# The first group's Q, K and V as plain products, in a two-layer graph network on one core

## The chip, the cores and the metric

The kernel runs on one NeuronCore of a Trainium2 chip. A core has TensorE (matrix products), VectorE (DVE, element work), ScalarE (ACT, activations and copies), GpSimd (POOL, element work too) and SyncE (SP), which here issues nearly all DMAs. Each engine runs its own instructions in order and waits on semaphores for the others. The metric is the device time of one execution in microseconds (us). Most executions agree within 0.3%.

## What is computed

The reference takes x with 128 batches of 128 rows and 512 features, and a 0/1 matrix of 128 x 128 for each batch. Layer 0 is attention with 8 heads; layer 1 is a graph attention with one score per pair of rows. After each comes the sum with its input and a layer norm. Everything is 32-bit.

```python
q = (inputs @ Wq + bq).reshape(bs, n, N_HEADS, HEAD_DIM)   # k, v likewise
logits = jnp.einsum('bqhd,bkhd->bhqk', q, k) / np.sqrt(HEAD_DIM)
attn = jax.nn.softmax(jnp.where(mask, logits, NEG_INF), axis=-1)
out = jax.nn.relu(jnp.einsum('bhqk,bkhd->bqhd', attn, v).reshape(bs, n, EMBED_DIM) @ Wo + bo)
x = layernorm(x + out)
Wh = x @ W
e = leaky(Wh @ a1 [:, None] + Wh @ a2 [None, :])            # masked, softmax over the first axis
x = layernorm(x + leaky(attention @ Wh))
```

## The kernel before

**Groups and chains.** Four batches form a group: its transposed input XT is 512 features by 512 rows. Q, K and V of a group are products of 512x512x512 each, and are not computed plainly: a scheme of the Strassen kind is used on two levels. The outer level splits each matrix in 2x2 blocks and needs 7 products instead of 8 (p1 to p7); the inner level does the same once more. So 49 products of 128x128x128 stand for 64. A name (Q, K, V) is done in two chains, of four and of three inner products per outer one. Chain c belongs to group c//6; c%6 is 0 and 1 for Q, 2 and 3 for K, 4 and 5 for V. LAST is the last chain.

**What the scheme needs.** Sums of input blocks: outer ones (`sum_x`, L523 to L526, on GpSimd) and inner ones (`inner_sum`, L500, on either engine). Sums of weight blocks: `Weights.build` (L302) gives eight steps, one for the inner 1, four outer ones (`right_blocks`, L259 to L262), then three inner ones (L291). Reading the products out of PSUM takes copies on ScalarE (`copy_out`, L694 to L700) and adds on VectorE (L715), and at the end of a chain three to six combines (`combine`, L731), each on the engine that its token names.

**Where things live.** The sums of wq stay in SBUF for the whole run. Those of Wk and Wv are built once in memory that other things need later (Wk's becomes that of wo and w1, Wv's is the arena), stored to DRAM (`stores`, L316) and streamed back for every later group through a ring of four tiles (`fetch_until`, L634). In group 0 the products read the blocks of all three in place.

**The opening.** x of the first two batches and Wq's first half are loaded first, then the rest (L1292 to L1304, L1389). VectorE and TensorE turn the rows of x; later inputs are loaded by `load_x` as blocks (four DMAs each, L421) and turned on VectorE (L426). Some transposes of the identity (`keep_busy`) run ahead of the first products. Q is scaled by 1/8 by scaling wq itself on VectorE (L1330, L1334), interleaved with the sums of wq and of the first inputs in a list of 25 steps (`opening`, L1369).

**Order.** The program has no scheduler: one order for all engines is written out as tokens. BEGIN covers the opening up to batch 5, STEADY repeats over the rest, PLAN is the end. Each token calls a method, and the instructions go to their engines in that order. `h` issues the next half step of the chains (one p and what reads it, reads being deferred), `a` and `d` the next deferred read on ScalarE and VectorE, `k` and `k.v` the next combine on GpSimd or VectorE, `q` one more streamed weight, `i1.s1a` an inner sum of group 1 (with .v on VectorE), `g1.0` an outer sum. `s0.` tokens are the softmax of batch 0: scores (L875), masked add (L889), maxima (L898), exponentials (L909), division (L923), a store to DRAM and a fetch back that reorders it (L930, L936), the turn (L942) and the product with V (L955). `z` is the rest of layer 0 for a pair of batches, `b4.` loads and turns of batch 4, `w.` the loads and sums of wo and w1. All of SyncE's DMAs leave in this order too, each only when its data and its target are free.

The half steps come from `sequence` (L605), which starts at chain 0 before the change; the result of a chain is written into one fixed tile for each of Q, K and V (`outputs`).

Of the kernel before, what the change touches and what calls it, by code (L numbers as in the profile page):

```python
# [20 lines left out]
BIG = -1e30  # L21

BEGIN = """
    b4.load.1 h o.0 b0.masks o.2 a o.1 o.3 o.6 h o.4 o.8 o.7 o.9 o.5 o.10 wk.build.0 d o.11
    o.12 o.17 wk.build.1 o.13 o.18 o.15 wk.build.2 o.16 o.14 o.19 o.20 wk.build.4 wk.build.3
    h h o.23 o.21 o.24 o.22 a h a wk.build.5 d wk.build.7 wv.build.0 h h h h wv.build.1 a
    wv.build.2 d k.v wk.store.0 h k.v b6.load.0 b1.cast a k.v k.v k.v k.v h a wk.store.1
    b5.load.2 h a b0.cast b4.turn d q w.bias h wk.build.6 d wv.build.3 b2.masks b7.load.1
    wk.store.3 h h h a h wv.build.4 a a wk.store.2 h h h a b3.cast a b0.mask d k.v b1.mask
    k.v k.v d b6.turn d h h h a b2.cast z1.by b7.turn k.v wv.build.5 h a h h h d b5.turn k.v  # L30
    d a a wv.build.6 wv.build.7 g1.0 d g1.1 g1.2 k.v k.v h h h h d a h k.v q q wv.store.2
    w.load b8.load.2 wv.store.1 b4.masks w.w1_load.1 wv.store.0 wv.store.3 k.v k.v d a h
    s0.scores a s0.add.0 k.v s0.add.1 d s0.reduce s2.scores h h s1.scores g1.3 a h h h h
    w.block.0 a s0.exp.0.1 s0.exp.4.5 d s1.add.1 i1.s1a i1.s1b.v s0.exp.2.3 a b4.cast
    s0.exp.6.7 i1.s2a s0.reciprocals.0 d s1.add.0 b2.mask s0.reciprocals.1 s1.reduce h k a
    s0.divide.2.3 s0.divide.4.5 s0.divide.0.1 s0.divide.6.7 s1.exp.7 h d s2.add.1
    w.w1_load.0 b9.load.0 b10.load.1 s3.scores h h a w.w1_load.3 w.w1_load.9 q s0.store
    w.w1_load.7 a z0.by s1.exp.3.4 b3.mask i1.s2b.v k.v k.v i1.s4a s1.exp.0.1 h h s1.exp.5.6
    a s1.exp.2 s3.add.1 d k.v k.v k.v k w.w1_load.6 b1.residual w.w1_load.5 s0.fetch
    w.w1_load.2 w.w1_load.8 h h s3.add.0 s1.reciprocals.1 s2.add.0 s1.reciprocals.0 d  # L40
    s1.divide.4.5 s2.reduce b8.turn i1.s3a i1.s4b i1.s3b h s1.divide.6.7 b5.cast a
    s1.divide.0.1 s1.divide.2.3 d h h a h h a s3.reduce b10.turn s1.store w.w1_load.4
    b0.residual b11.load.2 b2.residual s1.fetch s2.exp.6.7 s2.exp.2.3 s2.exp.4.5 q d
    s0.transpose w.block.1 a s2.exp.0.1 s3.exp.7 h h h d a k.v k.v s2.reciprocals.0
    s2.reciprocals.1 w.w1_sum.1 b4.mask d w.w1_sum.6 h s2.divide.6.7 s2.divide.0.1 a a
    s3.exp.2 s0.attend h h h s2.divide.2.3 s2.divide.4.5 w.block.3 w.w1_sum.2 s3.exp.5.6 d
    w.w1_sum.3 k.v a s0.copy w.halve s1.transpose s3.exp.3.4 z1.bw h h z0.p1 d
    s3.reciprocals.1 b9.turn w.block.2 w.w1_sum.4 k k k s3.exp.0.1 a s1.attend s1.copy h h
    z0.p2 s2.store d k k q s3.reciprocals.0 k.v q s1.sum.0 a s3.divide.7 a z0.t0
    s3.divide.0.1 s3.divide.5.6 b11.turn s1.sum.1 s1.sum.2 s2.fetch h h q h z0.p6 h  # L50
    s3.divide.2 s3.divide.3.4 q s3.store k.v d q w.w1_sum.0 k.v k q s3.fetch b3.residual q a
    z0.t2 z0.bw h a z0.p5 z0.p7 s2.transpose z0.t3 s1.sum.3 g2.0 b12.load.2 d d q g2.1 h
    z0.p4 q q w.w1_sum.9 h h a a w.w1_sum.8 z0.c22 k.v z0.p3 z0.c21 z0.c11 d b5.mask
    z0.stats.1 h z0.c12 k k.v h s2.attend s4.scores h z0.stats.0 s3.transpose s3.attend k
    g2.2 s2.copy a k z0.rstd.1 z0.rstd.0 s3.copy s4.add.1 s4.add.0 s4.reduce h a d
    z0.apply.1 d s5.scores h h h s4.exp.2.3 s4.exp.6.7 z1.p1 h s5.add.0 s5.add.1 s4.exp.0.1
    s4.exp.4.5 a a h g2.3 s3.sum.2 z0.apply.0 s4.reciprocals.1 s4.reciprocals.0 h d
    s5.reduce i2.s1a i2.s2a.v k.v d s4.divide.2.3 s3.sum.0 s3.sum.1 s4.divide.0.1
    s4.divide.4.5 s4.divide.6.7 z1.t0 a h q z0.store.1 q b6.masks z0.store.0 s5.exp.6.7
    s5.exp.3.4 s5.exp.2 a s5.exp.5 s5.exp.0.1 z1.p6 z1.p2 w.w1_sum.5 i2.s3a.v w.w1_sum.7  # L60
    i2.s1b.v k.v z1.t2 i2.s2b d h h h s4.store z0.fetch_both z1.p5 z1.p7 s5.reciprocals.1
    s5.reciprocals.0 z1.c11 s4.fetch a a s5.divide.2 h h s5.divide.7 s5.divide.5.6
    s5.divide.0.1 s5.divide.3.4 k.v z1.t3 d a b7.cast k.v k.v b12.turn w.w1_sum.10 z1.p4 h
    z1.c22 s4.transpose s3.sum.3 k k i2.s4a i2.s4b w.w1_block.0 s4.attend z1.p3 h h
    z0.transpose.0 z1.c21 z0.transpose.1 z1.stats.1 z1.rstd.1 i2.s3b z0.sum.0 d w.w1_sum.11
    s5.store a w.w1_block.1 z0.sum.1 q z1.c12 d s5.fetch h h z1.stats.0 s5.transpose h
    b6.cast a a s4.copy b13.load.0 d b13.turn b14.load.2 q z1.apply.1 k.v s5.attend s5.copy
    z1.rstd.0 w.w1_block.3 z0.sum.2 w.w1_block.2 k s5.sum.0 s5.sum.1 k z0.sum.3 s5.sum.2
    z1.store.1 b6.mask b7.mask s5.sum.3
"""  # L70

STEADY = {
# [96 lines left out]
def kernel(  # L169
# [293 lines left out]
    def sum_x(g, n):  # L463
        if g not in x_sums:
            begin_sums(g)
        x_sums[g][n]()
# [136 lines left out]
    LAST = 6 * (B // GROUP) - 1  # L603

    def sequence():  # L605
        steps = [(0, name) for name in ("p1", "p2", "p5", "p6")]
        for c in range(LAST + 1):
            steps.append((c, "p7"))
            follow = c + 1 <= LAST
            steps += [(c + 1, "p1")] if follow else []  # L610
            steps += [(c, "p4"), (c, "p3")]
            steps += [(c + 1, name) for name in ("p5", "p6", "p2")] if follow else []
        return steps
# [44 lines left out]
    def group_product(c):  # L658
# [6 lines left out]
            return ps_st.tile([P, 4, P], F32, name=f"st_{role}", tag=tag)[:, :count, :]  # L665

        def weight(n, m):
            if name == "Q" or g == 0:
                return {"Q": wq, "K": wk, "V": wv}[name].inner(m)[:, PLACE[n], :]
            return ring[c, f"p{n + 1}"][:, (0, 1, 2, 0, 3, 1, 2)[m], :]  # L670

        def multiply(p, n, start):
# [102 lines left out]

    def split_step():

        if steps_done[0] >= min(len(all_steps), 42 * (B // GROUP) - 13):
            return
        c, name = all_steps[steps_done[0]]  # L780
        steps_done[0] += 1
        half_step(c, name, True)
        if name == "p3":
            combos.extend(combine(c, comb_engine(c)))
# [3 lines left out]
            INNER[g][0](name, (None, "rest")["ab".index(part)], engine=engine)  # L788

    def comb_engine(c):  # L790
        return nc.vector if c % 6 in (3, 5) or c < 4 else nc.gpsimd

    def pair_product(xs, w, add, home, bias=None, bank=None):

# [531 lines left out]
            nc.tensor.transpose(p[:, c, :], turned[:, c * P : (c + 1) * P], ident)  # L1326
        copy(XT[0][:, :, b * P : (b + 1) * P], p)

    def scale(n):
        nc.vector.tensor_scalar_mul(wq.place(n), wq.place(n), QSCALE)  # L1330

    def scaled_less(n, left, right):

        nc.vector.scalar_tensor_tensor(  # L1334
            wq.place(n), wq.place(left), QSCALE, wq.place(right), op0=ALU.mult, op1=ALU.subtract
        )

    wq_sums = right_blocks([wq.place(n) for n in range(7)])
    begin_sums(0)
    x_inner = INNER[0][0]  # L1340
    turned = [order_features(b) for b in range(2)]
    keep_busy(14)
    transpose_rows(0, turned[0], nc.vector.tensor_copy)
# [1 line left out]
    transpose_rows(1, turned[1], nc.scalar.copy)  # L1345
    turn_biases()
    keep_busy(5)
    scale(0)
    scale(1)
    wq.first(nc.vector, 0, 2)()  # L1350
    x_inner("s1", 0, engine=nc.vector)
    wq.second(nc.vector, 0, 2)()
    x_inner("s2", 0, engine=nc.vector)

    ordered = {}

    def order(b):
        return lambda: ordered.update({b: order_features(b)})

    def rows(b):  # L1360
        return lambda: transpose_rows(b, ordered[b], nc.scalar.copy)

    def sum_of_x(n):
        return lambda: sum_x(0, n)

    def inner_of_x(name, half, engine=None):
        return lambda: x_inner(name, half, engine=engine)

    opening = [  # L1369
        order(2),  # L1370
        rows(2),
        order(3),
        rows(3),
        wq.first(nc.vector, 2, 4),
        lambda: scaled_less(2, 2, 0),
        *[sum_of_x(n) for n in range(4)],
        lambda: scaled_less(5, 3, 2),
        *wq_sums[2:],
        lambda: scale(3),
        wq.second(nc.vector, 2, 7),  # L1380
        inner_of_x("s1", 1, nc.vector),
        inner_of_x("s2", 1, nc.vector),
        inner_of_x("s1", "rest", nc.vector),
        inner_of_x("s2", "rest", nc.vector),
        *wq.others(nc.vector),
        *[inner_of_x(name, half) for name in ("s3", "s4") for half in (None, "rest")],
    ]

    load_blocks(Wv, columns(wv.blocks()), nc.sync)  # L1389
    END = B - GROUP  # L1390
# [28 lines left out]

    class Matrix:  # L1420
        def __init__(self, name, w, engine):
            self.builds = w.build(engine)
            self.stores = w.stores(stored[name, 0], stored[name, 1])

        def build(self, n):
            self.builds[n]()
# [62 lines left out]
    jobs.update({f"z{n}": LayerZero(n) for n in range(2)})  # L1489
    jobs.update({f"b{b}": Batch(b) for b in range(16)})  # L1490
    jobs.update(wk=Matrix("wk", wk, nc.vector), wv=Matrix("wv", wv, nc.gpsimd), w=Late())
    for token in BEGIN.split():
        if token[:2] == "o.":
            opening[int(token[2:])]()
        elif token[0] in "ig" and token[1] in "12":
            g = int(token[1])
            if token[0] == "i":
                common("i" + token[2:], g)
# [224 lines left out]
```

## Time and profile before

| | us |
|---|---|
| median of 3 runs | 2327.47 (2327.29 to 2330.24) |
| the profiled execution | 2328.13 |
| its span in the profile | 2325.5 |
| granted TensorE clock, mean | 0.993 |
| first product of group 0 (L681) | at 8.4 |
| scores of batch 0 (L875) | at 68.1 |
| first product of group 1 (L681) | at 77.4 |
| stores of Wk issued | 31.4 to 52.8 |
| stores of Wv issued | 55.6 to 70.0 |

Each engine's busy time is the union of its instructions; a busy TensorE is not one at its peak, since its products are pipelined and their ends are modelled. Idle time matters only where the chain that ends last passes through it. Times of single instructions are from one profiled execution. The DMA share is the mean busy share of the core's 16 DMA engines.

### The profile page before, as it was taken

Reading aid. Unit: us, or ns where it says so; the run is one execution under the profiler, and the core shown is the slowest. Engines: PE = TensorE matmul, PEld = TensorE weight load, DVE = VectorE, ACT = ScalarE, POOL = GpSimd, SP = SyncE. Lnnn points to the kernel's source line nnn. Section 1 sums busy time; section 2 is a strip of 40 time slices with the busy share of each in tenths; the row PEclk is TensorE's granted clock in tenths of the full one; section 3 lists DMA queues with packets and bytes.
Section 4 is the critical chain, followed back from the end, with each engine's and each line's share of the span. In section 5 each row is a group of like instructions: output and inputs, shape, how many; then the busy total and the mean of one; then the engine's idle time right before and its main releaser. Section 6 shows DMA issues by size and latency. Waiting matters only on the chain.

```text
span 2325.5 us, 53031 instructions
## 1 busy us (share of the span) xinstructions
PE 2264.5 (97%) x17394; PEld 2028.0 (87%) x17394; DVE 2116.6 (91%) x4248; ACT 1665.8 (72%) x5971; POOL 1465.7 (63%) x1735
## 2 busy tenths in 40 slices
PE   5999999999999999999999999999999999999998
PEld 5888988888988888889889889889888889888885
DVE  7998999999999999999999999999999999999977
ACT  1766776777777867767767767767767777777686
POOL 4466666667666666666676666676656666666656
PEclk7999999999999999999999999999999999999999
DMA  6978888888888888878888888888888888888774
GB/s 160 269 209 234 238 249 233 233 232 243 242 241 238 230 236 243 242 240 236 225 246 233 250 238 231 233 240 236 247 238 232 234 244 236 243 238 227 221 217 145
DMA packets 516595, 540.81 MB, mean 233 GB/s; under 512 B 100568, under 2 KB 394336, under 8 KB 516320
## 3 DMA queue, kind: packets, MB, share of 16 engines
q1 hardware_dynamic: 516000, 537.17, 80.8%
q8 instruction: 138, 2.26, 0.4%
q14 instruction: 137, 1.12, 0.2%
q10 hardware_dynamic: 320, 0.26, 0.0%
HBM read 388.96 MB, written 148.31 MB: 231 GB/s over the span
## 4 chain that ended last, share of the span: by engine, by line
PE 58%; DVE 19%; DMA 8%; POOL 5%; SPq 4%; issue 3%; ACT 3%; DVEq 0%; POOLq 0%; ACTq 0%
PE p_y L801 14%; PE st_y L681 14%; PE p_w L801 6%; PE lg L875 6%; PE st_w L681 6%; PE st_x L681 5%; DMA w_n<-wv 4%; DVE pa L942 4%; PE p_x L801 4%; PE p_oT L955 3%; DVE arena L1047 2%; DVE cells L715 2%; PE p_h L1211 2%; DVE st L1003 2%; DMA paz<-pa_dram 2%
## 5 line engine op out<-in xcount | busy, mean ns | idle before, releaser
L909 ACT ACTIVATE pa<-pa,nmax 128x128 f32<-128x128 f32 x1000 | 391.7, 398 | 1.9 <-DVE nmax L898 1.8
L923 ACT ACTIVATE pa<-pa,rs 128x128 f32<-128x128 f32 x1000 | 329.0, 398 | 15.4 <-DVE rs L919 15.2
L1009 POOL TENSOR_SCALAR ve<-mv 128x1 f32<-128x1 f32 x256 | 77.9, 304 | 288.6 <-DVE mv L1005 226.3
L694 ACT COPY cells<-st_y 128x384 f32<-128x384 f32 x288 | 136.2, 473 | 115.8 <-PE st_y L681 102.9
L1024 DVE TENSOR_SCALAR arena<-arena,mv,rstd 128x512 f32<-128x512 f32 x239 | 185.5, 776 | 14.3 <-POOL rstd L1011 14.3
L909 ACT ACTIVATION_READ_ACCUMULATOR pa<-pa,nmax 128x1 f32 x1000 | 194.9, 195 | 0.0
L970 ACT ACTIVATE arena<-p_oT,b_cols 128x128 f32<-128x128 f32 x504 | 144.2, 370 | 64.5 <-PE p_oT L955 60.5
L523 POOL TENSOR_TENSOR x1S<-x1T 128x256 f32<-128x256 f32 x62 | 57.6, 928 | 208.2 <-DVE mf L853 208.2
L1011 POOL TENSOR_TENSOR rstd<-ve,mhalf 128x1 f32<-128x1 f32 x256 | 160.6, 627 | 21.4
L1003 DVE BATCH_NORM_STATS2 st<-arena 128x6 f32<-128x512 f32 x248 | 168.0, 677 | 1.1
L942 DVE STREAM_TRANSPOSE pa<-paz 128x1024 f32<-128x1024 f32 x125 | 154.6, 1237 | 9.6 <-DMA paz<-pa_dram 7.7
L889 DVE TENSOR_TENSOR pa<-lg,mf 128x512 f32<-128x512 f32 x250 | 161.2, 675 | 0.9 <-PE lg L875 0.9
L955 PE MATMUL p_oT<-pa,out_V 128*64 128x128 f32 x2000 | 136.7, 279 | 18.7 <-DVE pa L942 18.7
L694 ACT COPY out_V<-st_y 128x512 f32<-128x512 f32 x128 | 74.5, 582 | 109.5 <-PE st_y L681 109.0
L875 PEld LDWEIGHTS lg<-out_K,out_Q 64*128 64x128 f32 x2048 | 124.2, 187 | 31.9 <-issue 20.4
L875 PE MATMUL lg<-out_K,out_Q 64*128 64x128 f32 x2048 | 148.7, 285 | 0.8 <-DVE out_K L731 0.8
L898 DVE TENSOR_REDUCE nmax<-pa 128x8 f32<-128x1024 f32 x125 | 148.4, 1187 | 0.1
L955 PEld LDWEIGHTS p_oT<-pa,out_V 128*64 128x64 f32 x2000 | 106.7, 136 | 42.0 <-DVE pa L942 33.7
L801 PE MATMUL p_y<-wo_w,x1S 128*128 128x257 f32 x496 | 134.3, 393 | 0.1
L1218 ACT ACTIVATE arena<-p_h 128x512 f32<-128x512 f32 x120 | 71.5, 596 | 87.1 <-DMA out_dram<-arena 59.3
L715 DVE TENSOR_TENSOR cells<-st_w,cells 128x384 f32<-128x384 f32 (+1 forms) x224 | 126.7, 566 | 6.5 <-PE st_w L681 2.9
L801 PE MATMUL p_y<-wo_w,x1T 128*128 128x257 f32 x496 | 131.6, 387 | 0.4 <-ACT arena L812 0.4
(296 smaller groups left out, 7960.2 us busy)
## 6 DMA issues: line engine op xcount, KB each, us to landing
paz<-pa_dram SPq DMA_DIRECT2D x504, 128.0 KB, 3.5
pa_dram<-pa SPq DMA_DIRECT2D x125, 512.0 KB, 3.8
w_n<-wk SPq DMA_DIRECT2D x93, 512.0 KB, 5.9
w_n<-wv SPq DMA_DIRECT2D x93, 512.0 KB, 5.0
w_n<-wk SPq DMA_DIRECT2D x93, 384.0 KB, 4.3
w_n<-wv SPq DMA_DIRECT2D x93, 384.0 KB, 5.6
x_dram<-arena SPq DMA_DIRECT2D x128, 256.0 KB, 2.8
xz<-x_dram SPq DMA_DIRECT2D x240, 128.0 KB, 4.2
```

The costliest lines, as they stand in the source:

```text
L681: nc.tensor.matmul(p[:, index, :], lhs, rhs, start=start and index == 0, stop=True, skip_group_check=True,)
L694: nc.scalar.copy(dst, p)
L715: nc.vector.tensor_add(cells(c)(h, o), p, t)
L801: nc.tensor.matmul(p[:, :width], xs()[n][:, kc, :], w[:, PLACE[n], kc, :], start=start and kc == 0, stop=True, skip_group_check=True,)
L875: nc.tensor.matmul(self.lg[r][:, c, :], q[rows, 2 * (b % 2) + c % 2, c // 2, :], k[rows, 2 * (b % 2) + c % 2, c // 2, :], start=c == 0, st ...
L889: nc.vector.tensor_add(by_head[:, r * NC : (r + 1) * NC], self.lg[r].rearrange("p c (b k) -> p c b k", b=4), mf.unsqueeze(1).to_broadcast( ...
L909: nc.scalar.activation(self.pa[:, :, h, :], self.pa[:, :, h, :], AF.Exp, bias=self.nmax[:, h : h + 1], accum_out=self.sums[:, h : h + 1],)
L923: nc.scalar.activation(self.pa[:, :, h, :], self.pa[:, :, h, :], AF.Copy, scale=self.rs[:, h : h + 1])
L942: nc.vector.transpose(self.paT.rearrange("p h (a i) -> p a h i", i=32), self.paz.rearrange("p a (h k) -> p a h k", k=32),)
L955: nc.tensor.matmul(self.oT[r * HD : (r + 1) * HD, c, :], v[:, c % 2, c // 2, r * HD : (r + 1) * HD], self.paT[:, r * NC + c, :], start=c == 0,
L1003: nc.vector.bn_stats(st, self.src)
L1024: nc.vector.tensor_scalar(self.src, self.src, self.mv[:, 0:1], self.r, ALU.subtract, ALU.mult)
```

## The change

Group 0 no longer goes through the scheme. Its Q, K and V are plain products of the weights as loaded: for Q four output blocks in two halves of 256 columns (`q`), for K four of 512 columns (`k`), for V four batches of 512 columns (`v`). A copy on ScalarE reads each out (`oq`, `ok`, `ov`); Q's copy scales and adds the bias. After Q, wq is scaled in place on ScalarE and its sums are built on VectorE by the same `build` that the others use. The chains begin at chain 6, so 42 half steps go, with the input sums of group 0. BEGIN is written anew: it has 501 tokens instead of 590, with `y.` tokens for the plain products and `wq.` tokens for the scaling and the sums. STEADY and PLAN are as they were.

```diff
     def sequence():
-        steps = [(0, name) for name in ("p1", "p2", "p5", "p6")]
-        for c in range(LAST + 1):
+        steps = [(6, name) for name in ("p1", "p5", "p6", "p2")]
+        for c in range(6, LAST + 1):
...
-        if steps_done[0] >= min(len(all_steps), 42 * (B // GROUP) - 13):
+        if steps_done[0] >= min(len(all_steps), 42 * (B // GROUP - 1) - 13):
...
     def comb_engine(c):
-        return nc.vector if c % 6 in (3, 5) or c < 4 else nc.gpsimd
+        return nc.vector if c % 6 in (3, 5) else nc.gpsimd
...
+    class Group:
...
+        def bank(self, key, n):
+            if key not in self.p:
+                self.p[key] = (
+                    ps_st.tile([P, D], F32, name=f"st_{'ywx'[n]}", tag="abc"[n])
+                    if n < 3
+                    else psum("p_first")
+                )
+            return self.p[key]
+
+        def turned_product(self, name, w, n, cols, start):
+            o, j = divmod(n, 2)
+            p = self.bank((name, n), n)
+            for c in range(NC):
+                block = w.place(2 * o + c // 2).rearrange("p (c f) -> p c f", c=2)
+                nc.tensor.matmul(
+                    p[:, cols],
+                    block[:, c % 2, j * P : (j + 1) * P],
+                    XT[0][:, c, cols],
+                    start=start and c == 0,
...
+        def q(self, n, half):
+            self.turned_product("Q", wq, n, slice(half * 2 * P, (half + 1) * 2 * P), half == 0)
+
+        def oq(self, n):
+            def copy(dst, p, n):
+                nc.scalar.activation(
+                    dst, p, AF.Identity, bias=b_cols[:, 0, n : n + 1], scale=QSCALE
+                )
...
+        def k(self, n):
+            self.turned_product("K", wk, n, slice(0, D), True)
...
+        def v(self, b):
+            p = self.bank(("V", b), b)
+            blocks = wv.low.rearrange("p n (c j) f -> p n c (j f)", c=2)
+            for c in range(NC):
+                nc.tensor.matmul(
+                    p.rearrange("p (o f) -> p o f", o=2),
+                    XT[0][:, c, b * P : (b + 1) * P],
+                    blocks[:, c // 2 : 4 : 2, c % 2, :],
...
     class Matrix:
...
+        def scale(self, n):
+            nc.scalar.mul(self.w.place(n), self.w.place(n), QSCALE)
...
+    jobs.update(wq=Matrix("wq", wq, nc.vector), y=Group())
```

The first tokens of the new BEGIN, up to the first half step of group 1:

```
y.order.3 y.q.0.0 y.order.2 b0.masks y.q.1.0 y.rows.2 y.rows.3 b4.load.1 b6.load.0
b5.load.2 w.bias b2.masks y.q.2.0 y.q.2.1 y.q.1.1 y.oq.1 y.k.3 y.k.1 y.k.2 b4.turn
b1.cast y.q.3.0 y.q.0.1 b0.cast y.oq.2 b7.load.1 y.q.3.1 b1.mask wk.build.0 b6.turn
b5.turn wk.build.1 b3.cast b0.mask wk.build.2 wk.build.3 y.ok.2 b2.cast wq.scale.0
y.oq.0 wq.scale.1 wq.scale.2 y.ok.1 y.ok.3 wq.scale.3 wk.build.4 wk.build.5 y.k.0 y.ok.0
y.oq.3 s0.scores wk.build.6 b7.turn wk.build.7 b2.mask b3.mask s1.scores g1.0 g1.2
...
s0.exp.0.1 s0.exp.6.7 b4.cast s0.exp.4.5 i1.s1a.v wk.store.2 y.v.1 wk.store.3 s0.exp.2.3
b5.cast q q y.v.0 y.v.2 y.v.3 i1.s3a.v s1.reduce wq.build.4 s0.reciprocals.0
s0.reciprocals.1 s0.divide.4.5 s0.divide.2.3 i1.s2a wq.build.3 i1.s4a.v wq.build.5
s1.exp.5.6 s0.divide.0.1 h
```

## The prediction

> **What bounds the kernel now.** I read the page first, then the windows of 20 us, then the waits of TensorE, then the chain of waits, then the timelines of the opening.
>
> The page's busy times and slices:
> ```profile
> PE 2264.5 (97%) x17394; PEld 2028.0 (87%) x17394; DVE 2116.6 (91%) x4248; ACT 1665.8 (72%) x5971; POOL 1465.7 (63%) x1735
> ...
> PE   5999999999999999999999999999999999999998
> ...
> PEclk7999999999999999999999999999999999999999
> ```
> TensorE is the bound everywhere except in the first slice of 58 us, where it is half idle and its granted clock is low. Whatever shifts the moment at which TensorE is kept full shifts the end. The windows (busy of PE, PEld, DVE, ACT, POOL, then clock, DMA share, GB/s) say how far the opening reaches:
> ```profile
> 0.00:20.00 20.00, 9.93 (x57) 8.10 (x57) 10.97 (x22) 3.92 (x8) 7.17 (x11) 0.87 0.86 201
> 20.00:40.00 20.00, 11.34 (x62) 10.37 (x62) 19.86 (x21) 3.34 (x11) 15.85 (x10) 0.70 0.54 146
> 40.00:60.00 20.00, 12.98 (x90) 12.86 (x91) 15.72 (x20) 5.13 (x12) 7.51 (x4) 0.74 0.52 152
> ...
> 80.00:100.00 20.00, 16.55 (x142) 15.14 (x141) 19.20 (x46) 18.56 (x77) 8.63 (x8) 1.00 1.00 231
> 100.00:120.00 20.00, 18.57 (x147) 17.21 (x147) 17.88 (x43) 11.80 (x39) 10.88 (x11) 1.00 0.96 272
> ```
> Two stages: up to 60 us TensorE waits and VectorE is full from 20 us on while the DMA engines are half idle; from 80 us VectorE is full and the DMA share is at 1. The waits of TensorE up to 77.4 us (the end of the first group's V) name the causes:
> ```profile
> PE st_y L681 <- ACT cells L694: 9.7, 1, 9.7
> PE st_w L681 <- DVE inner_s L500: 5.3, 1, 5.3
> PE st_w L681 <- DVE wq L291: 2.6, 1, 2.6
> PE st_w L681 <- DMA wo_w<-in_L_gnn_Wk_dram: 2.4, 1, 2.4
> ```
> The 9.7 us is a VectorE wait in disguise, as the chain shows: the copy waits for the combines of Q (L731).
> ```profile
> 36.97 5.05 DVE out_Q L731 x4
> ...
> 44.09 2.30 DVE out_Q L731
> 46.49 0.49 ACT cells L694
> 47.02 4.64 PE st_y L681 x20
> ...
> 91.61 6.45 DMA xz<-in_x_dram
> 98.08 4.86 DMA paz<-pa_dram
> 103.06 1.25 DVE pa L942
> ```
> Later in the same chain transfers end last: the fetch of the softmax of batch 1 goes out at 95.19 and VectorE gets it at 103.06.
>
> **What the Trainium skill says.** "TensorE: Matmul & The Clock Gate", section "What's actually happening": TensorE has two clocks, half rate after an idle window, full after about 3.4 us of sustained work. The trace agrees: the 5-us windows show 1.00 up to 15 us, 0.50 from 15 to 30 and from 45 to 50, each time after a wait. "SBUF — State Buffer", section "Who interferes with whom": a VectorE instruction with two SBUF inputs and a GpSimd one that reads SBUF block each other. It agrees: two 128x256 combines took 0.87 us at 94.59 with GpSimd idle, and three took 3.58 us at 36.16 with GpSimd full. "DMA: Bandwidth & Descriptors", section "Issuing engines are not separate DMA queues": all issues share 16 engines. Here that shows as the 4.86 us that a 128-KB fetch took beside the weight traffic.
>
> **The change part by part.**
> *Where both programs meet again.* The remaining order of every engine is identical from TensorE instruction 470 (387 in the changed program), VectorE 225 (176) and DMA issue 160 (160). In the trace these points lie at 148.9 us, 157.3 us and about 152 us. I call them the joint; 42 half steps (six chains) go, and the steady loop starts at the same step. So the question is by how much the joint moves.
>
> *TensorE's own work rises.* A 128-column product is two records at 0.222 us (eight st_x records 0.89 us in the chain), a 256-column one 0.43 us (four p_y records 0.86), a 512-column one 0.86 us (two p_h records 0.86). Out: 6 chains with 147 products, 32.6 us. In: 32 of 256 and 32 of 512 columns, 13.8 + 27.5 = 41.3 us. Cost 8.7 us at full clock.
>
> *TensorE's waits in the opening go.* The first product is possible when Wq's first half lands, 7.9 us (where L1330 starts now). Two products groups of 4x0.43 give 11.4; eight transposes 12.3; Wq's second half is there at 12.8 (VectorE's wait ends then); three groups of 1.73 give 18.0; Wk is there by 17.6. Three K groups of 3.45 give 28.4, three Q halves 33.6. K 0 needs the bank that the Q 0 copy frees, and on ScalarE that copy stands behind the first in-place scaling of wq, which must wait for the last Q read: scaling 0.5 and copy 0.6, so K 0 starts at 34.8 and ends at 38.3; two more copies 39.6. Both scores (1.09 each) 41.8, V 16x0.86 = 13.8: 55.6 us. TensorE never rests for long, so I take full clock. Now the same point is 77.4. TensorE is 22 us ahead, with one score product (1.1 us) less done.
>
> *VectorE.* 49 instructions fewer up to the joint: 42 adds of L715 and L731 (0.42 to 0.69 us alone) and five scalings of wq go, two block sums for wq come: some 27 us less. Ten input turns, Wk's builds and wq's builds remain. First stop: the input of batch 4, which is issued after Wv, adj (18.6) and lands near 22.5 us. From there turns (0.7 each) and eight Wk builds (0.69, four of 0.68, three of 1.05) run to 35 us; wq's scaling ends at 37.5; builds, two masked adds and maxima of two batches (0.68, 0.68, 1.2), sums of group 1 beside GpSimd: 54.8 us. Then it waits for V's end (batch 8's turn takes the buffer of the first group's input) and for the score of batch 2: the first add into group 1's Q comes at 60.5 us. It comes at 86.57 now. From there to the joint I count 122 instructions against 123, of the same kinds within 1 us. That stretch is 70.7 us long, and VectorE was busy for 97% of it. Were VectorE alone the limit, the joint would come at 131, 26 us earlier.
>
> *The DMA queue.* Bytes are unchanged: 33 MB up to the joint. SyncE issues in order. Six input batches now go before the first Wk store; that store needs five builds, 30.4 us (31.4 now), the other three by 34.8 (now 52.8). wo and W1 share Wk's memory, so their loads wait for the stores to be read, about 44. Wv's builds overwrite the blocks that the V products read, so GpSimd starts them at 55.8 and takes 15.3 us (as at 30.79 to 46.09 now): 71.1. The queue waits for them twice, at its first Wv store (64) and its last (71.1); behind that stand the fetch of batch 1's softmax, residuals, streamed weights and the store of batch 2. Batch 1's fetch thus leaves at 71 (95.19 now), still 24 us early, but from 64 on Wv's stores, batch 1's store and the fetch bring 4.2 MB, 15.7 us at 270 GB/s: landing near 80 where VectorE would want it at 77. Behind it 3.4 MB to batch 2's fetch, 12.7 us: 92.7 against 86; batch 3, 2.2 MB more, 101 against 97. So transfers are late by 4 to 7 us. I take 6. (From 60 to 155 us the trace moves 244 GB/s at a share of 88%, so 276 at a full one; I take 270.) The total says the same: 33 MB at 270 GB/s is 122 us, to which the early gaps (about 8 us) and some later ones come; a joint at 131 leaves nothing over.
>
> *Other edits.* ScalarE takes 12 copies of 128x512 (0.6) and 4 scalings (0.5) and loses 32 smaller ones (0.31 to 0.59): about 5 us less, and it is idle for half of this stretch. The edit of comb_engine does nothing: chains below 4 are no longer stepped, and each combine's engine stands in its token. GpSimd's sums for group 0 (eight at 1.4 to 2.1 us) go, those for group 1 move ahead of Wv's builds.
>
> *Sum.* 26 minus 6: the joint 20 us earlier. Behind it TensorE is the bound (98% busy from 157 to 297 us), so the lead stays. The profiled execution took 2328.13, its span 2325.5; it lies 0.7 above the median of 2327.47. 2328.1 - 20 = 2308, from the median 2307.5.
>
> The costs not shown: a Q scaling on ScalarE of 128x512 from SBUF has no row; between 0.4 (VectorE's L1330) and 0.6 (copies from PSUM), I take 0.5: 4 of them, at most 0.4 us either way. The late transfers are 0 to 14 us (nothing excludes that the queue holds further issues back). TensorE's clock in the opening: if it falls to half for one stretch as it does now, 3 to 5 us; if not, 0, which I take.
>
> **Rivals.**
> 1. *Transfers keep up.* For it: the store of Wk leaves 15 us earlier and the half-idle DMA from 20 to 60 us is filled. Against it: shares of 1 between 80 and 125. The joint moves 26 us: 2301.5.
> 2. *The DMA queue becomes the bound.* For it: SyncE is stopped four times (Wk stores, wo's memory, batch 8's turn, Wv stores) and the traffic is squeezed from 152 into about 130 us. Then two thirds of the lead go, and 8 us remain: 2319.5.
> 3. *Nothing to see.* The joint is held at about 148 by the total of transfers with gaps of 26 us: 2325.
> 4. *Slower.* The queue stands at the last Wv store, which waits for GpSimd, which waits for V and shares its port with a full VectorE. Batch 1's fetch, now issued at 95.19, stands behind. Wv's builds would have to take 40 us instead of 15.3 (each doubled and more by VectorE's lock) for this to decide; each us later than 95 costs one: with 50 us of builds 2338. Against it: with GpSimd full VectorE is what suffers in the trace (3.58 us for three combines), the builds took 1.3 to 2.2 us each.
>
> That the sums are not built meanwhile is excluded by the order: TensorE has both scores and V between k and the first group-1 product.
>
> **How the numbers follow.** The forecast, 20 us off with its own range of 2303 to 2313, has 0.47; rival 1 0.21, rival 2 0.21, rival 3 0.05, rival 4 0.06. A measurement of this kernel tells 0.2%, 4.7 us, from no change. Faster: 0.47 + 0.21 + 0.21 = 0.89; same 0.05; slower 0.06. The range runs from 2299, rival 1 with 2.5 us to spare, to 2320, which takes in most of rival 2.
>
> **What would show it.** Right: the first plain product at 8 us and V's end near 56; the first score near 40; clock 1.00 from 8 us on; the last Wv store at about 71; VectorE's first add into out_Q near 60; the joint on VectorE near 137; waits on fetches of paz between 75 and 105. Wrong: TensorE at half clock from 15 to 40 us, a first score after 50, Wv stores after 80, or a joint later than 148; and a lead at the joint that is lost again before 300 us would refute that TensorE bounds what follows.

## The result and the profile after

| | before | after |
|---|---|---|
| median of 6 runs, us | 2327.34 (2325.08 to 2330.24) | 2306.28 (2304.29 to 2309.14) |
| profiled execution, us (span) | 2328.13 (2325.5) | 2304.29 (2302.5) |
| first product of group 0 / first score / end of group 0's V, us | 8.4 / 68.1 / 81.2 | 7.8 / 37.6 / 53.6 |
| first product of group 1, us | 77.4 | 54.9 |
| first add into group 1's Q, us | 86.57 | 60.99 |
| joint on VectorE (first masked add of batch 6), us | 158.2 | 133.3 |

The ratio of the medians is 0.991, with a 95% interval of 0.9898 to 0.9923: 21 us less, 18 to 24 by the interval. The forecast was 2307.5.

The page of the changed kernel, busy times and slices:
```profile
PE 2265.1 (98%) x17228; PEld 2013.5 (87%) x17228; DVE 2076.6 (90%) x4199; ACT 1661.2 (72%) x5955; POOL 1443.9 (63%) x1723
...
PE   9899999999999999999999999999999999999998
...
PEclk9999999999999999999999999999999999999999
```
TensorE's busy time is the same as before to 0.6 us, although its granted clock is now full from the start; VectorE has 40 us less to do. The first slice went from 5 to 9 tenths (the second from 9 to 8): the gain is there. The windows (us, busy of PE, PEld, DVE, ACT and POOL with their instructions, clock, DMA share, GB/s) show it more closely:
```profile
0.00:20.00 20.00, 18.09 (x85) 14.68 (x86) 2.75 (x9) 3.82 (x6) 0.72 (x7) 1.00 0.87 204
20.00:40.00 20.00, 19.32 (x85) 11.42 (x84) 13.16 (x18) 6.88 (x15) 4.90 (x4) 1.00 0.79 217
40.00:60.00 20.00, 18.13 (x74) 9.77 (x73) 16.75 (x27) 12.09 (x50) 11.97 (x8) 1.00 1.06 290
...
80.00:100.00 20.00, 19.90 (x167) 18.30 (x168) 18.20 (x48) 12.14 (x38) 10.01 (x10) 1.00 0.93 304
100.00:120.00 20.00, 18.23 (x138) 15.49 (x138) 19.56 (x47) 16.41 (x64) 12.18 (x15) 1.00 0.70 202
```
In the first 60 us TensorE and VectorE have changed places: TensorE is busy for 55.5 us (34.3 before), VectorE for 32.7 (46.6 before). The waits of TensorE in the first 56 us answer to the 9.7, 5.3, 2.6 and 2.4 us of before:
```profile
PE p_busy L1320 <- POOL ident masks.py:199: 1.3, 1, 1.3
PE st_y L681 <- ACT out_V L1416: 1.3, 1, 1.3
PE lg L875 <- ACT out_K L1395: 0.7, 1, 0.7
PE st_y L1364 <- DMA wq<-in_L_gnn_Wq_dram: 0.4, 1, 0.4
```
No wait for VectorE is left among them. What ends last now is in the chain of waits (start, length, what; the long steps up to batch 1's attention):
```profile
17.78 5.71 DMA adj<-in_adj_dram
...
26.29 4.22 DMA adj<-in_adj_dram
...
36.56 8.64 DMA wk<-wo_w
...
46.21 5.53 DMA wo_w<-in_L_gnn_Wo_dram
51.76 6.73 DMA wo_w<-in_L_gnn_W_dram
...
63.20 6.74 DMA wv<-arena
...
74.25 4.53 DMA paz<-pa_dram
78.80 1.26 DVE pa L942
80.10 1.09 PE p_oT L955 x16
```
Before, this stretch of the chain was VectorE's combines and TensorE's products. Now each long step up to 78.8 us is a transfer, and the last Wv store and batch 1's fetch stand in it, as the forecast's part on the DMA queue had them. Behind the joint the lead was kept: batch by batch, VectorE's transpose of the softmax (L942) comes 23.8 to 25.4 us earlier from the fifth to the 124th of 128, and 23.0 us earlier for the last four.

### The profile page after: what moved, and what is told of

Its sections match the earlier page's. It is cut to its first block, busy times and chain, and to the rows that moved or that the text cites. A ratio compares the mean times of both kernels' runs of the same rounds, so it can differ in the third digit from the quotient of the medians.

```text
span 2302.5 us, 52596 instructions
## 1 busy us (share of the span) xinstructions
PE 2265.1 (98%) x17228; PEld 2013.5 (87%) x17228; DVE 2076.6 (90%) x4199; ACT 1661.2 (72%) x5955; POOL 1443.9 (63%) x1723
## 4 chain that ended last, share of the span: by engine, by line
PE 58%; DVE 19%; DMA 9%; POOL 6%; SPq 3%; issue 3%; ACT 2%; DVEq 0%; POOLq 0%; ACTq 0%
PE p_y L801 14%; PE st_y L681 13%; PE lg L875 6%; PE p_w L801 6%; PE st_w L681 6%; PE st_x L681 5%; DVE pa L942 4%; PE p_x L801 4%; DMA w_n<-wv 3%; PE p_oT L955 3%; DVE arena L1047 3%; DVE cells L715 2%; DVE st L1003 2%; PE p_h L1211 2%; DVE arena L1024 2%
## 5 line engine op out<-in xcount | busy, mean ns | idle before, releaser
L923 ACT ACTIVATE pa<-pa,rs 128x128 f32<-128x128 f32 x1000 | 329.2, 397 | 14.4 <-DVE rs L919 14.3
L942 DVE STREAM_TRANSPOSE pa<-paz 128x1024 f32<-128x1024 f32 x125 | 154.5, 1236 | 8.5 <-DMA paz<-pa_dram 6.1
L1218 ACT ACTIVATE arena<-p_h 128x512 f32<-128x512 f32 x120 | 71.5, 596 | 87.8 <-DMA out_dram<-arena 60.5
L801 PE MATMUL p_y<-wo_w,x1S 128*128 128x257 f32 x496 | 134.3, 393 | 0.2
L801 PE MATMUL p_y<-wo_w,oS 128*128 128x256 f32 x504 | 129.8, 380 | 0.4 <-ACT y L812 0.4
```

Source lines behind the costliest of these rows:

```text
L801: nc.tensor.matmul(p[:, :width], xs()[n][:, kc, :], w[:, PLACE[n], kc, :], start=start and kc == 0, stop=True, skip_group_check=True,)
L923: nc.scalar.activation(self.pa[:, :, h, :], self.pa[:, :, h, :], AF.Copy, scale=self.rs[:, h : h + 1])
L942: nc.vector.transpose(self.paT.rearrange("p h (a i) -> p a h i", i=32), self.paz.rearrange("p a (h k) -> p a h k", k=32),)
```

## The experiments

How much two numbers may differ before it means something: the changed kernel was profiled twice, with the joint at 133.3 and 135.0 us, spans of 2302.5 and 2304.9 us, and medians 21.1 and 20.3 us under before's on the same chip. I take 20.7 us as its gain. A joint under 3 us away, or a median under 2 us away, says nothing. In the table "cost" is 20.7 less the kernel's own gain over before beside it.

| run | edit | median | before beside it | ratio (95%) | joint | cost, us |
|---|---|---|---|---|---|---|
| e1 | +8.7 us TensorE, opening | 2313.94 | 2328.33 | 0.9935 (0.9921 to 0.9950) | 143.3 | 6.3 |
| e2 | +8.7 us TensorE, middle | 2312.15 | 2328.33 | 0.9930 (0.9914 to 0.9947) | 139.7 | 4.5 |
| e3 | +8.4 us VectorE, middle | 2317.12 | 2328.33 | 0.9947 (0.9932 to 0.9961) | 144.3 | 9.5 |
| e4 | +2.3 MB of stores, middle | 2312.14 | 2328.33 | 0.9926 (0.9911 to 0.9941) | 141.2 | 4.5 |
| e5 | +12.7 us VectorE, opening | 2306.60 | 2329.49 | 0.9911 (0.9894 to 0.9927) | 136.2 | -2.2 |
| e6 | before, clock held up | 2327.74 | 2329.49 | 0.9994 (0.9986 to 1.0003) | 159.4 | |
| e7 | before, no combines of group 0 | 2322.01 | 2329.49 | 0.9964 (0.9951 to 0.9977) | 149.9 | |
| e8 | the changed kernel | 2308.47 | 2328.80 | 0.9913 (0.9900 to 0.9927) | 135.0 | 0.4 |
| e9 | two waits moved away | 2308.05 | 2328.80 | 0.9910 (0.9896 to 0.9923) | 140.1 | 0.0 |
| e10 | and loads moved back | 2309.50 | 2328.80 | 0.9912 (0.9899 to 0.9926) | 138.0 | 1.4 |
| e11 | -7.9 us VectorE, middle | 2306.02 | 2327.11 | 0.9908 (0.9892 to 0.9925) | 137.0 | -0.4 |
| e12 | no Wv stores (-3.1 MB) | 2304.63 | 2329.42 | 0.9893 (0.9876 to 0.9909) | 131.6 | -4.1 |

**What held the opening before: two runs from the kernel before.** The rival to "VectorE's sums" was TensorE's low clock, 0.70 and 0.74 between 20 and 60 us. Run e6 fills the waits with transposes:
```
+                if c == 0 and n == 4 and index < 3:
+                    keep_busy((12, 40, 18)[index])
+                if c == 1 and n == 6 and index == 0:
+                    keep_busy(80)
```


> The kernel before, with idle-filling transposes (as its warm-up has them) inside the waits of TensorE's opening: 12, 40 and 18 ahead of the first three inner products of the first chain and 80 ahead of the second chain's last products, so that TensorE's granted clock stays up there. Nothing is left out. Theory 'the opening before is VectorE's chain of sums, and TensorE only waits in it': 0 to 3 us faster than before, since products at full clock wait for the same sums. Rival 'the opening before is slow because TensorE runs at a lower clock in it': 8 us faster or more, a good part of the change's 21. If the transposes overrun the waits, up to 5 us slower.

The windows of e6:
```profile
20.00:40.00 20.00, 14.88 (x102) 13.92 (x101) 19.17 (x20) 3.35 (x11) 15.36 (x10) 0.84 0.50 143
40.00:60.00 20.00, 20.00 (x176) 19.79 (x176) 16.96 (x23) 5.13 (x12) 8.05 (x4) 0.99 0.47 132
```
The clock rose to 0.84 and 0.99, VectorE stayed about as busy (19.2 and 17.0 us, against 19.9 and 15.7), and the first score came at 67.7 us in place of 68.1. The time did not move (ratio 0.9994, interval 0.9986 to 1.0003). The fillers were not free: the last row of 80 ran until 49.1 us, although the copy that the next product needs was done by 47.8, so up to 1.3 us may be hidden. But that copy was no earlier than before (47.0), so VectorE's sums ended where they had ended. In this opening the low clock was a sign of the waits and cost next to nothing by itself. Further on this is not so, as the runs below show.

Run e7 takes away a part of VectorE's sums instead:
```
-            combos.extend(combine(c, comb_engine(c)))
+            combos.extend([lambda by=None: None] * len(combine(c, comb_engine(c))) if c < 6 else combine(c, comb_engine(c)))
```


> The kernel before, with the sums that put the seven products of group 0 together into Q, K and V left out (24 of them on VectorE; the group's Q, K and V keep what they were filled with once, so attention of the first four batches is computed from other numbers). The sums of inputs and weights stay. Theory 'VectorE's work in the opening sets when group 1 starts': TensorE's wait of 9.7 us for a combined block goes, 8 to 14 us faster than before, more than half of the change's 21, the rest of the gain being the inputs' and weights' sums. Rival 'TensorE's products of the opening set it': the products are the same, so 0 to 4 us faster.

It gained 7.5 us by the medians (0.36%, interval 0.23 to 0.49%), a little under the 8 to 14 expected and less than half of the change's gain, where more than half was expected. Its lead over before is 8 us at the first transposes and 6.7 at the last. Much more work than that went: of the 24 sums left out the trace of before has 22 on VectorE, and they took 22.0 us there. VectorE's busy time up to the joint fell from 138.7 to 120.9 us. So less than half of the removed work came back as time, and the rest became waiting. The waits of TensorE that remain in e7:
```profile
PE st_w L682 <- DVE inner_s L500: 5.2, 1, 5.2
PE st_w L682 <- DVE cells L716: 3.8, 2, 2.4
...
PE st_w L682 <- DVE wq L291: 2.6, 1, 2.6
```
The wait of 9.7 us is gone, those for the inputs' and the weights' sums stand as before, and the one for VectorE's adds (L716) has grown from 1.3 to 3.8 us. So the combines account for a good third of the change's gain. That the inputs' and weights' sums account for the rest is what these lines suggest; it is not shown, since a kernel before without them was not run. TensorE's clock in e7 was 0.72 between 20 and 40 us; whether it costs something once the combines are gone was not run either.

**What holds the opening now: e1 and e5.** Both add idle work to the changed kernel's hand-written order, through jobs of this kind:
```
+        def dve(self, n):
+            for _ in range(n):
+                nc.vector.tensor_add(scratch, wq.place(0)[:, :HALF], wq.place(1)[:, :HALF])
+        def pe(self, n):
+            keep_busy(n)
```
Run e1 has `t.pe.79` ahead of `y.k.3`, the first product of K; e5 has `t.dve.30` ahead of `b0.masks`.

> The changed kernel with 79 transposes of the identity (0.11 us each, 8.7 us) on TensorE between Q's and K's plain products. If TensorE sets the opening (the theory on record), the end of V moves from 53.6 to about 62 us, and since VectorE takes the first score 3.4 us after it is there, the meeting point on VectorE (133.3 us) moves by 5 to 8.7 us: 2311 to 2315 us. If the DMA queue set the lead, the delay would be hidden: at most 2308.

> The changed kernel plus 30 dead VectorE sums of 128x256 (12.6 us of VectorE's time by the 0.42 us of such a row) put just before the masks of batch 0, at about 10 us, where VectorE otherwise stands idle from 10.4 to 24.4 us for the input of batch 4. Theory 'what counts is the stretch after V, and in the opening VectorE has time to spare': at most 1 us slower than the changed kernel, joint at 133 to 134 us. Rival 'the gain is VectorE's total work, wherever it lies': 10 to 12 us slower, joint at about 144 us. In the middle stretch the same kind of sums (20 of them, 8.4 us) cost 10 us, so a near zero here shows that the place decides.

With e5 nothing was lost: 30 sums of 0.42 us each lay where VectorE waits for batch 4's input. This line of the changed kernel's VectorE timeline has that wait, 13.97 us, in its brackets:
```profile
24.38 0.71 DVE L426 STREAM_TRANSPOSE xT<-xz 128x512 f32<-128x512 f32 x1 [13.97 <-DMA xz<-in_x_dram]
```
So VectorE's total is not what the change sells; the removed sums pay only as far as they stood ahead of group 1. With e1 the first score came at 46.9 us, 9.2 later, the joint at 143.3. VectorE's waits for TensorE in the first 60 us of e1 show how this reaches it; Wk's builds overwrite the blocks that the K products read:
```profile
DVE wo_w L291 <- PE st_x L1364: 11.0, 1, 11.0
```
In the changed kernel the same line has 2.4 us. Of 8.7 us added, 6.3 reached the end, so TensorE has at most a few us of room in the opening, and VectorE follows it. The chain of waits shown above puts transfers last in the same stretch (17.8 to 58 us). No run took transfers away there, so which of the two comes last in the unedited kernel is open.

**What holds the middle, from V's end to the joint: e2, e3 and e4 add.** The same amounts are spread over four places (ahead of `s1.fetch`, `s0.copy`, `s2.fetch` and `s2.attend`): 79 transposes, 20 sums, or five stores of 0.46 MB that nobody reads.

> The same 79 transposes in four parts between 70 and 110 us instead. If VectorE's work sets the middle stretch, TensorE has room there and the cost is at most 3 us: 2306 to 2309. If TensorE is the bound there too, all 8.7 us: 2315. If transfers set it: at most 2.

> The changed kernel with 20 dead sums of 128x256 (0.42 us each alone, 8.4 us) on VectorE in four parts between 70 and 110 us. If VectorE's work sets the middle stretch (the theory on record), 5 to 8.4 us: 2311 to 2315. If TensorE or the transfers set it, at most 3: 2306 to 2309.

> The changed kernel with five dead stores of 0.46 MB (2.3 MB, 8.5 us at 270 GB/s) on the DMA queue in four parts between 70 and 110 us. If transfers set the middle stretch (the rival that the DMA queue becomes the bound), 6 to 8.5 us: 2312 to 2315. The forecast charged 6 us for late transfers, so it would give about the same. If VectorE sets it and the transfers are only just in time, 1 to 4: 2307 to 2310.

VectorE's work counted nearly in full, 9.5 us for 8.4 planned: its sums took 0.426 us in the median, but up to 1.375 beside GpSimd, 10.6 us together. But transfers (2.3 MB, 8.3 us at the prediction's 276 GB/s) and TensorE cost 4.5 us each, and the joint moved by 5 to 8 us in both; "VectorE alone sets the middle" had allowed neither so much. VectorE's waits of e4 between 56 and 145 us:
```profile
DVE pa L942 <- DMA paz<-pa_dram: 5.2, 1, 5.2
DVE pa L889 <- PE lg L875: 4.7, 1, 4.7
DVE wa_scr L382 <- DMA arena<-in_L_gnn_a_dram: 2.1, 1, 2.1
```
In the changed kernel these three are 2.6, 3.1 and 0.5 us. The transfers have no room that would hide 8 us more: about half of it shows in the time, in part by way of TensorE's clock (see below).

**And e9 to e12 take away.** Run e9 puts the score of batch 2 right behind V's products and V's copies earlier; e10 also moves three loads behind batch 0's fetch, and Wv's loads behind batch 5's:
```
-    b5.cast q q y.v.0 y.v.2 y.v.3 i1.s3a.v s1.reduce wq.build.4 s0.reciprocals.0
+    b5.cast q q y.v.0 y.v.2 y.v.3 s2.scores i1.s3a.v s1.reduce wq.build.4 s0.reciprocals.0
...
-    s1.reciprocals.0 s2.add.0 wv.build.0 wv.build.1 b11.load.2 w.w1_load.1 w.w1_load.0
-    s0.fetch wv.build.2 s1.divide.4.5 s1.divide.6.7 h wv.build.3 wv.build.4 s1.divide.0.1 a
+    s1.reciprocals.0 s2.add.0 wv.build.0 wv.build.1     s0.fetch b11.load.2 w.w1_load.1 w.w1_load.0 wv.build.2 s1.divide.4.5 s1.divide.6.7 h wv.build.3 wv.build.4 s1.divide.0.1 a
```


> The changed kernel itself, as control beside the next two on the same chip: 20 to 22 us faster than before, joint at about 133 us.

> The changed kernel with three products of TensorE earlier in its order: the scores of batch 2 right after V's last product, and V's copies to the places from which attention reads a little earlier in ScalarE's order. Theory 'the middle stretch is VectorE's chain, so its waits are worth their length': VectorE's wait of 3.1 us for that score and TensorE's of 1.3 us for the copy go, joint at 130 to 132 us, 1 to 3 us faster than the control. Rival 'transfers end last in that stretch': the waits go and come back at the next fetch, 0 to 1 us.

> As the one before, and on the DMA queue also the loads of W1's last two blocks and of batch 11 moved behind the fetch of batch 0's attention, and Wv's loads behind batch 5's. If transfers end last in the middle stretch: 3 to 6 us faster than the control. If VectorE does: as the one before, 1 to 3 us, since its waits for such transfers sum to 2.6 us there. A loss would mean that Wv's later load delays the products of V.

Neither gained. VectorE's wait of 3.1 us for the score is gone in e9, and this stands in its place (56 to 140 us):
```profile
DVE pa L942 <- DMA paz<-pa_dram: 4.4, 2, 2.8
DVE out_Q L715 <- ACT out_Q L700: 2.1, 1, 2.1
DVE out_K L715 <- ACT out_K L694: 1.7, 1, 1.7
```
(The joint of e9 is that of its longest execution, 2311.0 us; its shortest took 2305.5.) In e10 batch 0's fetch left SyncE no earlier (61.6 us against 60.8), since it waits for its own store, and batch 1's left at 74.7 in place of 71.3, behind batch 11's and W1's loads (63.5 to 66.3), which had been moved between the two: the queue was only put in another order.

Run e11 leaves out VectorE's own share of the combines of group 1, twelve sums before the joint:
```
             def run(by=None):
+                if 6 <= c < 12 and (by or engine) is nc.vector:
+                    return
```


> The changed kernel with those sums left out by which VectorE puts the products of group 1 together (Q, K and V of batches 4 to 7 then come out of unfinished sums): twelve of 128x256 and 128x512 lie before the joint, 7.9 us of VectorE by their rows; GpSimd's part of these sums stays, and so do products and transfers. Theory 'VectorE alone limits the middle stretch': 7 to 9 us faster than the changed kernel, joint at 125 to 127 us, ratio to before about 0.988. Rival 'VectorE, transfers and TensorE are all nearly full there, so adding to any of them costs but taking from one alone brings little': 0 to 4 us faster, joint at 130 to 133 us, waits for paz or for products in the place of the sums.

7.9 us of VectorE's work went and 0.4 us came back, which cannot be told from nothing. Its waits from 56 to 134 us (line numbers below the edit are two higher in this kernel):
```profile
DVE pa L891 <- PE lg L877: 4.6, 1, 4.6
DVE pa L944 <- DMA paz<-pa_dram: 4.0, 1, 4.0
DVE out_K L715 <- ACT out_K L694: 2.0, 1, 2.0
DVE out_K L715 <- PE st_w L681: 2.0, 1, 2.0
```
Batch 1's softmax came at 80.9 us, no earlier than with the sums (78.8 and 80.7 in the two profiles of the changed kernel), and the saved time became waiting. Part of it went another way. TensorE waited 3.1 us for that softmax, and its next products ran at half the clock: the window from 80 to 100 us shows 0.83, where the changed kernel has 1.00. First the two lines of the changed kernel's chain, then those of e11:
```profile
80.10 1.09 PE p_oT L955 x16
81.19 1.76 PE st_y L681 x14
```
```profile
82.17 1.97 PE p_oT L957 x16
84.14 3.29 PE st_y L681 x14
```
From batch 1's product with V to batch 2's it was 15.6 us in the changed kernel (80.10 to 95.72), 15.5 in the control and 18.3 in e11 (82.17 to 100.47). So some 2.7 us went to the clock, and without them the joint would lie near 134.3 (an estimate from these figures), still not earlier than in the changed kernel. With that the theory that VectorE alone limits the middle has fallen, though a gain of up to 3 us may be hidden.

The same holds for other runs. In the windows of 5 us from 40 to 160 us the clock is full in the changed kernel, e1, e2 and e12. It is 0.66 in one window in the control and in e5, and the lowest windows show 0.50 to 0.76 in e3, e4, e9 and e10. In e4 TensorE waited 5.3 us for batch 1's softmax, and from that product to batch 2's it was 18.4 us, 2.8 more than in the changed kernel. So of the 4.5 us that the stores cost, more than half can be this. So each single execution holds some us that its edit alone does not set.

Run e12 asks the same of the transfers. Wv's stores go, and the later groups read K's blocks as V's:
```
-            src = stored["w" + chain_name(c).lower(), r][low : high + 1 : max(high - low, 1)]
+            src = stored["wk", r][low : high + 1 : max(high - low, 1)]
...
         def store(self, n):
-            self.stores[n]()
+            if self.w is wk:
+                self.stores[n]()
```


> The changed kernel with the four stores of Wv's built blocks left out (3.1 MB, between 62.8 and about 78 us, and with them SyncE's waits for GpSimd's builds); V of batches 4 and later then reads the blocks of Wk's store in their place, as many bytes. All builds, sums and products stay. In the changed kernel's chain of waits every long step from 17.8 to 78.8 us is a transfer, the last two of them the Wv store and batch 1's fetch of paz. Theory 'transfers set the opening and the middle up to that fetch': batch 1's softmax reaches VectorE 4 us or more earlier (at 75 us or before), joint at 128 to 131 us, 3 to 6 us faster than the changed kernel. Rival 'three engines share the stretch, and relief of one gives way to the next': the fetch comes earlier, but the joint at 132 to 135 us, 0 to 2 us faster. Rival 'the stand of SyncE is covered': no change in the fetch either.

It gained 4.1 us on the changed kernel. By the two ratios alone that is at the edge of what can be told (their intervals overlap). All four of its runs, 2302.19 to 2305.24, lie below all five of the control, 2306.74 to 2310.09, but not below the first six of the same kernel, which begin at 2304.29. The window of e12, and VectorE's waits from 56 to 134 us:
```profile
60.00:80.00 20.00, 17.77 (x166) 16.14 (x165) 17.52 (x35) 16.73 (x64) 13.60 (x10) 1.00 0.70 204
```
```profile
DVE pa L889 <- PE lg L875: 3.1, 1, 3.1
DVE pa L942 <- DMA paz<-pa_dram: 1.6, 1, 1.6
```
The DMA share there fell from 0.97 to 0.70 and TensorE was busy 2.4 us longer than the 15.37 us of the changed kernel. Batch 1's fetch left SyncE at 69.1 us in place of 71.3, and VectorE took it at 76.7 without waiting for it; the expectation had been 75 or before. The joint came at 131.6, 26.6 us earlier than before, and 1.7 and 3.4 us earlier than in the two profiles of the changed kernel. The joint alone would say little by the rule above; with the earlier fetch and the times of the four executions the direction is likely, and the size is not settled.

The edit also takes away two things at once: the bytes, and SyncE's stand for GpSimd's builds. In the changed kernel SyncE waits 1.7 us for a build and after that 1.1 us more for batch 1's own store to land before it can fetch, which speaks for the bytes. And it leaves ScalarE in place: in e12 SyncE waits 2.9 us for ScalarE's division of batch 1 before it can store (at 66.4), and in the changed kernel ScalarE is busy for 5.97 of the 6 us before that store (60 to 66). ScalarE is a fourth engine on this path, and no run relieved it.

Taken together: in the middle TensorE, VectorE and the transfers each have only a few us of room. Adding to any of them costs half of it or all. Taking from VectorE alone gave nothing that can be told, because the transfers stood right behind and TensorE's clock fell; taking from the transfers gave 2 to 4 us, with ScalarE and VectorE next.

## Why the prediction was right

- *TensorE's work rises by 8.7 us and its waits go.* Right. A group of eight 512-column records took 3.43 us (17.70 to 21.13), 0.86 a product as priced. First product 7.8 us (forecast 7.9), first score 37.6 (39.6), V's end 53.6 (55.6). Of the 2 us, 1.4 are from K's last product: it started at 33.4 in place of 34.8. The forecast had the first scaling of wq wait for the last Q product; it began at 31.4, before that product ended (33.4), and the copy behind it came in time. A scaling took 0.63 us, just above the bound of 0.4 to 0.6, and nobody waited for it. One reading was wrong: at 77.4 us the first product of group 1 starts before the change, while group 0's V ends at 81.2. By the first product of group 1 TensorE came 22.5 us earlier, by V's end 27.6. No term of the sum rests on it.
- *Clock.* It was 1.00 up to the joint, as taken. Run e6 adds that the low clock of before was not a cost of its own.
- *VectorE.* Right in its places: batch 4's input at 24.4 (22.5), Wk built at 35.9 (35), the first add into group 1's Q at 61.0 (60.5). The 27 us of removed work were too few: up to the joint VectorE was busy for 138.7 us before and 98.5 after, 40 us less for the same 49 instructions, since the sum had priced them at what they take alone and many had run beside GpSimd (busy for 88.5 us before, 63.1 after). No term of the forecast hung on it, and e5 shows why: 12.7 us more of VectorE in the opening change nothing. What carries the gain there is the earlier start of group 1, for which TensorE has little room (e1). And the stretch from the first add to the joint had been read as 97% busy; the trace has 67.2 of 70.7 us, 95%.
- *DMA queue.* Right: Wk's stores 32.8 to 39.3 us (30.4 to 34.8), the loads behind them from 45.3 (44), Wv's builds from 53.7 and 14.4 us long (55.8 and 15.3), the last Wv store issued from 68.5 to 70.0 (71.1), batch 1's fetch issued at 71.3 (71), taken at 78.8 (80).
- *The late transfers: the term that was mis-sized.* The prediction took 6 us off 26 for them. From the first add into group 1's Q to the mark of the joint it was 71.6 us before and 72.3 after (73.5 in the control), so 0.7 to 1.9 us were lost there, and the joint came 24.9 us earlier (23.1 in the control), not 20. Against before's times less 26 us, the transposes of batches 1, 2 and 3 were late by 1.7, 5.1 and 2.2 us (78.80, 91.00 and 99.20 against 103.06, 111.88 and 123.00), where the prediction had 3, 7 and 4. So the lateness of single fetches was nearly as forecast; the error was to carry the worst of it to the joint, where most of it had been made up. What the traffic itself costs is seen in e12: without the Wv stores the joint came 1.7 to 3.4 us earlier.
- *The lead stays.* Right in kind: TensorE was busy for 99.3 of the 100 us from 200 to 300. 24.9 us at the joint became 23.0 between the spans and 21 between the medians. The step from 24.6 to 23.0 can be placed. In both kernels TensorE waits 2.0 us for the softmax of the 124th batch. The windows behind that wait are (changed kernel first, kernel before second):
```profile
2210.00:2215.00 5.00, 5.00 (x39) 4.21 (x36) 3.47 (x5) 2.38 (x8) 2.65 (x4) 0.66 0.27 102
```
```profile
2235.00:2240.00 5.00, 5.00 (x55) 4.56 (x52) 4.23 (x6) 4.16 (x16) 2.66 (x4) 1.00 0.36 117
```
The clock is at 0.66 in the one and at 1.00 in the other. The profiles of the control, e2, e9 and e10 have the same step of 1.5 to 1.6 us there, those of e1, e3, e4, e11 and e12 have not, so it belongs to the execution and not to the change. The profiled execution was the fastest of six; how much of the remaining 2 us is loss and how much is the spread of executions is not settled. The joint came 3 to 5 us earlier than forecast, and 3 to 4 us were lost behind it, where the forecast had nothing (control and profiled execution). These two errors have opposite signs, and it is luck that the sum came closer than its terms.
- *Rivals.* "Transfers keep up" was 26 us: the change itself brought 21, and 24.8 only with Wv's stores left out (e12). "The DMA queue becomes the bound" named the mechanism that e4 and e12 show, but priced it at 18 us. "Nothing to see" had the joint held at 148 us by the traffic; it came at 133.3. SyncE behind slow Wv builds, the slower case, did not come: the builds took 14.4 us.

## What to carry to other kernels

Count the work that a change removes only as far as it stands ahead of what comes next: 12.7 us of VectorE put into a wait cost nothing, and the same sort of work further on cost nearly all of itself. When one engine gives way, work out where each of the others would end, and take the latest; if they lie within some us of each other, adding to any of them is expensive and relieving one alone brings little. Before a list of waits is tuned away, ask which wait stands behind each. And look at the clock of every edited run: an edit that makes TensorE wait in a stretch where it has little room can also slow the products behind the wait (2.7 us in e11), and this is easily taken for the cost of the edit.

## What was not expected of the hardware

- Issues of a fetch on SyncE's queue are not always short. The 32 issues of paz up to 180 us took 0.303 to 1.657 us with a median of 0.430; in the kernel before none of the 28 up to there took over 0.533. Batch 1's four took 3.44 us together, batch 0's 1.85. The change is not what brings it: over the whole execution the longest issue of paz took 2.10 us before and 1.85 after. Why is not shown.
- The same VectorE sum of 128x256 took 0.419 to 0.426 us thirty times over with GpSimd nearly idle (e5), and up to 1.375 us among GpSimd's sums (e3). The Trainium skill, "SBUF — State Buffer", section "Who interferes with whom", has a VectorE instruction with two SBUF inputs contend with a GpSimd one that reads SBUF. The factor is about three here. In the kernel before it was over five: three such sums (L731, from 39.7 us on) took 2.29 us each while GpSimd built Wv's sums.
